# Reordering the chunks around the y transform, and splitting the turn of two transform results between ScalarE and VectorE

## The chip, the cores and the metric

The kernel runs on one core of a Trainium2 chip. The time is device microseconds (us) from the first to the last instruction of one launch, and the time of a kernel is the median of several runs. The engines go by short names: PE is TensorE (matrix products), ACT is ScalarE, DVE is VectorE, POOL is GpSimd, and SP is the engine whose queue issues most of the DMAs. SBUF is the on-chip working memory of 128 partitions; PSUM is the memory that PE writes its results into.

## The reference, cut to what matters

The program is a Fourier neural operator of four layers over 64 images of 256 x 256 points and 32 channels, and one transformer layer behind it. The change touches only the first three Fourier layers.

```python
v = x @ p_w + p_b                                  # 64 images, 32 channels, 256 x 256
for i in range(4):
    x_ft = rfft2(v)                                # only 24 x 12 modes are kept
    x1 = irfft2(x_ft[kept modes] mixed by W1, W2)
    x2 = einsum('bcxy,cd->bdxy', v, w_w[i]) + w_b[i]
    v = x1 + x2
    v = (v - mean(v)) * rsqrt(var(v) + eps) * bn_g[i] + bn_b[i]
    if i < 3: v = relu(v)
out = einsum('bcxy,cu->bxyu', v, q_w) + q_b        # then attention and a feed-forward layer
```

The kernel does the transforms as matrix products with tables of cosines and sines. The mean and variance of layer i+1 are worked out ahead of it: the variance needs the sum of squares of `v @ w_w[i+1]`, which is why each layer also computes that product and sums its squares.

## The kernel before, in words

`layer(i, ...)` is called for i = 0, 1, 2. It loops over the 64 images `b`, and for each over 8 chunks `t` of the image. Four kinds of work are in the loop:

- **A chunk**, `pre(b, t)`: 8 products (L624) expand the inverse x transform `y_[b]` along y into two PSUM tiles; for i > 0, 16 products of 32 x 32 (L635) add the previous layer's values, loaded as `vin`. ACT applies relu to the first tile (L642) and DVE to the second (L643), both into the SBUF tile `vo`. SP stores `vo` (L644). DVE turns `vo` in 32 x 32 blocks into half of a tile `t32` (L647).
- **A product**, `product(b, t)`: 16 products of 32 x 32 (L659) of `vo` with the next layer's weights into two PSUM tiles, whose squares ACT sums (L666).
- **The forward transform** of image b: `along_y(b)` reads all four `t32` tiles of the image in 128 products (L676) into two PSUM tiles, and DVE turns both into `zt` (L686). `along_x(b)` makes 12 products out of `zt` (L699), ACT copies the result (L706) and SP stores it.
- **The inverse x transform** of the next image: `scale_am(b + 1)` on POOL (L594) and `spread(b + 1)`: four products (L605) into two PSUM tiles, which DVE turns into `y_[b + 1]` (L609).

In the trace each product of the source shows as two matmuls, so a product over 16 tiles is 32 instructions, `along_y` 256, L624 of a chunk 16.

PE runs one stage behind: chunk t, then the product of chunk t - 1. `along_y(b - 1)` stands behind the product at t = 1 of image b, `along_x(b - 1)` behind the product at t = 3, `spread(b + 1)` behind that at t = 5.

**Buffers.** All PSUM tiles of the layer come from one pool of four tiles named `ring`[...]: a chunk takes two, a product two, `along_y` two, `along_x` one, `spread` two. `t32` tiles come from the pool `lt` of five; an image needs four of them. `vin` and `vo` have four buffers each, `zt` one:

```python
(n, k) for n, k in (("lo", 4), ("ly", 2), ("la", 2), ("lc", 1), ("lx", 2), ("lz", 1), ("lt", 5))
pp = pool("lp", 4, space=PSUM)
```

A tile whose buffers are all taken waits until the last reader of an earlier tile of the pool is done.

**Order.** The layer runs inside `with tc.manual_schedule():`, so each engine issues its instructions in the order in which the program emits them; only the waits set how the engines stand to one another. An instruction that waits on an engine holds back all that stand behind it there.

Of the kernel before, what the change touches and what calls it, by code (L numbers as in the profile page):

```python
# [9 lines left out]
F32 = mybir.dt.float32  # L10
# [7 lines left out]
C = 32  # L18
# [117 lines left out]
def tile_fno_fusion_transformer(ctx: ExitStack, tc: tile.TileContext, a, cst_d, grid_d, out):  # L136
    nc = tc.nc
# [370 lines left out]
    def layer(i, st, src, dst, acc):  # L508
# [7 lines left out]
        with ExitStack() as cx:  # L516
# [69 lines left out]
            def load_v(b, t):  # L586
                vin[b, t] = ip.tile([128, 8, S], F32, name="vin")
                nc.sync.dma_start(vin[b, t], src[b][:, t])
# [8 lines left out]

            def spread(b):

                y_[b] = yp.tile([128, 2, 32, C], F32, name="y_")  # L600
                for h in range(2):
                    ps = pp.tile([128, 2, 512], F32, name="ring")
                    for n in range(2):
                        hv = slice(64 * n, 64 * n + rows_)
                        nc.tensor.matmul(  # L605
                            ps[:, n, :], lhsT=EX[hv, 128 * h:128 * h + 128], rhs=ams[b % 2][hv],
                            start=True, stop=True, skip_group_check=True,
                        )
                    nc.vector.transpose(  # L609
                        y_[b][:, h].rearrange("p q c -> p c q"),  # L610
                        ps.rearrange("p n (c k) -> p (n c) k", k=32),
                    )

            def four():

                t2 = [pp.tile([128, 2, 512], F32, name="ring") for _ in range(2)]
                return t2, [t2[n // 2][:, n % 2] for n in range(4)]

            def pre(b, t):
                t2, ps = four()  # L620
                for r in range(2):
                    for n in range(4):
                        q = 8 * (t % 4) + 4 * r
                        nc.tensor.matmul(  # L624
                            ps[n][:, 256 * r:256 * r + 256],
                            lhsT=y_[b][32 * n:32 * n + K, t // 4, q:q + 4, :].rearrange("p q c -> p (q c)"),
                            rhs=mv[b % 2][32 * n:32 * n + K, 2 * t + r, :] if i == 0 else T4[32 * n:32 * n + K, :],
                            start=r == 0, stop=i == 0, skip_group_check=True,
                        )
                if i:  # L630
                    v = vin.pop((b, t))
                    for k in range(4):
                        for n in range(4):
                            j = (n + k) % 4
                            nc.tensor.matmul(  # L635
                                ps[n][32 * j:32 * j + 32], lhsT=ws[32 * n:32 * n + 32],
                                rhs=v[32 * n:32 * n + 32, 2 * j:2 * j + 2, :], start=False, stop=True,
                                skip_group_check=True, tile_position=(32 * n, 32 * j),
                            )
                o = vo[b, t] = op.tile([128, 8, S], F32, name="vo")  # L640
                of = o.rearrange("p (n r) y -> p n (r y)", r=2)
                nc.scalar.activation(of[:, 0:2], t2[0], AF.Relu)  # L642
                nc.vector.tensor_scalar(of[:, 2:4], t2[1], 0.0, None, ALU.max)  # L643
                nc.sync.dma_start(dst[b][:, t], o)  # L644
                if t % 2 == 0:
                    t32[b, t // 2] = tp.tile([128, 8, 16, C], F32, name="t32")
                nc.vector.transpose(  # L647
                    t32[b, t // 2][:, :, 8 * (t % 2):8 * (t % 2) + 8, :].rearrange("p y s c -> p s y c"),
                    o.rearrange("p s (y l) -> p s y l", l=32),
                )  # L650

            def product(b, t):

                o = vo.pop((b, t))
                t2, ps = four()
                for k in range(4):
                    for n in range(4):
                        j = (n + k) % 4
                        nc.tensor.matmul(  # L659
                            ps[n][32 * j:32 * j + 32], lhsT=w4[i + 1][32 * n:32 * n + 32],  # L660
                            rhs=o[32 * n:32 * n + 32, 2 * j:2 * j + 2, :], start=True, stop=True,
                            skip_group_check=True, tile_position=(32 * n, 32 * j),
                        )
                for n in range(2):
                    at = 2 * (8 * b + t) + n
                    nc.scalar.activation(t2[n], t2[n], AF.Square, accum_out=acc[:, at:at + 1])  # L666
# [3 lines left out]
            def along_y(b):  # L670
                t2, ps = four()
                for k in range(8):
                    for m in range(4):
                        for n in range(4):
                            j = (n + m) % 4
                            nc.tensor.matmul(  # L676
                                ps[n][32 * j:32 * j + 32], lhsT=FYT[32 * n:32 * n + 32, k, :],
                                rhs=t32[b, j][32 * n:32 * n + 32, k].rearrange("p s c -> p (s c)"),
                                start=k == 0, stop=k == 7, skip_group_check=True,
                                tile_position=(32 * n, 32 * j),  # L680
                            )
                for j in range(4):
                    t32.pop((b, j))
                zt = zts[b] = zp.tile([128, 2, 32, C], F32, name="zt")
                for h in range(2):
                    nc.vector.transpose(  # L686
                        zt[:, h].rearrange("p k c -> p c k"),
                        t2[h].rearrange("p n (s c) -> p c (n s)", c=C),
                    )

            def along_x(b):
# [21 lines left out]
                for t in range(4):  # L713
                    load_v(0, t)
            scale_am(0)
            spread(0)
            for b in range(B + 1):
                for t in range(8):
                    if b < B:
                        pre(b, t)  # L720
                        nb, nt = (b, t + 4) if t < 4 else (b + 1, t - 4)
                        if i and nb < B:
                            load_v(nb, nt)
                    pb, pt = (b, t - 1) if t else (b - 1, 7)
                    if pb >= 0 and (b < B or t == 0):
                        product(pb, pt)
                    if b and t == 1:
                        along_y(b - 1)
                    if b and t == 3:
                        along_x(b - 1)  # L730
                    if b + 1 < B:
                        if t == 0:
                            load_am(b + 1)
                            if i == 0:
                                load_x(b + 1)
                        if t == 2:
                            scale_am(b + 1)
                        if t == 5:
                            spread(b + 1)

    st = None
    acc = None
# [405 lines left out]
```

## Time and profile before

| what | value |
| --- | --- |
| median of 3 runs | 12365.77 us (12355.73 to 12369.66) |
| the profiled execution | 12360.58 us, its span 12358.8 us |
| PE busy | 11164.5 us, 90% of the span |
| DVE busy | 8774.8 us, 71% |
| ACT busy | 6094.5 us, 49% |
| PE, layer 0 (200 to 3062 us) | busy 2599.55 of 2862.00 us |
| PE, layer 1 (3205 to 6326 us) | busy 2875.70 of 3121.00 us |
| PE, layer 2 (6470 to 9600 us) | busy 2883.83 of 3130.00 us |
| DMA share in those layers | 0.54, 0.90, 0.90 |

A line of a timeline gives start, duration, engine, source line, operation, output<-inputs, shapes and count, and in brackets the idle time of the engine before it and what ended it. `PEld` is PE's weight load. A line of the groups gives the total busy time and the mean duration of one instruction in ns behind the bar, and then the idle time before the group. A matmul's end is modelled in the profile, and consecutive matmuls overlap, so that the distance from one start to the next says more than the duration of one.

### The profile page before, as it was taken

To read this page: it belongs to the slowest core of one execution; us is meant where nothing else is said; L and a number is where in the kernel's file an instruction comes from. 1 tells how busy PE (TensorE), PEld (TensorE's weight loads), DVE (VectorE), ACT (ScalarE), POOL (GpSimd) and SP (SyncE) were. 2 spreads that over 40 slices of the span, in tenths; PEclk is the share of its full clock that TensorE was granted. 3 is DMA by queue.
4 is the path that set the end of the run, shared out by engine and by line. 5 is a ranking of instruction groups with operands and counts; after the bars stand their busy time and mean duration, and the time that the engine had idled before them with its cause. 6 is when DMAs were issued, how large, how long until landed. Compare 5 with 4: busy or idle time off the path is not lost. (4 is left out here: it accounts for less than half of the span.)

```text
span 12358.8 us, 405064 instructions
## 1 busy us (share of the span) xinstructions
PE 11164.5 (90%) x182038; PEld 5874.0 (48%) x182038; DVE 8774.8 (71%) x10667; ACT 6094.5 (49%) x10249; POOL 1412.7 (11%) x1987
## 2 busy tenths in 40 slices
PE   6999999998799999999979999999999699999999
PEld 3444444443444444444434444444444366666666
DVE  6777777777776777777766777767777566666665
ACT  5555555555555555555544555555555333333333
POOL 0000000000000000000010000000000133333333
PEclk8999999999899999999989999999999799999999
DMA  7555555555899999888889989889899755555554
GB/s 226 200 199 203 203 201 201 201 200 210 325 354 349 349 351 350 348 347 348 346 302 352 354 346 355 339 339 353 346 351 352 247 234 227 219 228 233 218 223 152
DMA packets 589283, 3485.06 MB, mean 282 GB/s; under 512 B 95000, under 2 KB 144536, under 8 KB 188568
## 3 DMA queue, kind: packets, MB, share of 16 engines
q1 hardware_dynamic: 539520, 3392.84, 71.2%
q0 software_dynamic: 40880, 62.59, 2.0%
q8 instruction: 1423, 23.31, 0.8%
q10 hardware_dynamic: 7144, 3.72, 0.1%
q14 instruction: 316, 2.59, 0.1%
HBM read 1761.87 MB, written 1696.92 MB: 280 GB/s over the span
## 5 line engine op out<-in xcount | busy, mean ns | idle before, releaser
L666 ACT ACTIVATE ring<-ring 128x1024 f32<-128x1024 f32 x3072 | 3108.8, 1012 | 1186.4 <-PE ring L659 1148.7
L647 DVE STREAM_TRANSPOSE t<-vo 128x2048 f32<-128x2048 f32 x1536 | 3550.0, 2311 | 175.1 <-ACT vo L642 14.5
L659 PE MATMUL ring<-vo,w 32*32 32x512 f32 x49152 | 2849.3, 622 | 392.2 <-DVE zt L686 138.7
L642 ACT ACTIVATE vo<-ring 128x1024 f32<-128x1024 f32 x1536 | 1568.2, 1021 | 2997.7 <-PE ring L635 2378.9
L643 DVE TENSOR_SCALAR vo<-ring 128x1024 f32<-128x1024 f32 x1536 | 1857.7, 1209 | 608.2 <-PE ring L635 420.4
L676 PE MATMUL ring<-t,cst 32*32 32x512 f32 x49152 | 1864.7, 601 | 303.7 <-issue 302.1
L686 DVE STREAM_TRANSPOSE zt<-ring 128x1024 f32<-128x1024 f32 x384 | 711.8, 1925 | 1658.6 <-PE ring L676 1658.6
L659 PEld LDWEIGHTS ring<-vo,w 32*32 32x32 f32 x49152 | 761.3, 105 | 1898.7 <-ACT ring L666 477.0
L676 PEld LDWEIGHTS ring<-t,cst 32*32 32x32 f32 x49152 | 975.9, 103 | 1157.0 <-issue 707.8
L594 POOL TENSOR_TENSOR ams<-am,sk 48x512 f32<-48x512 f32 x384 | 486.9, 1268 | 8642.4 <-DMA am<-mix 8039.9
L635 PE MATMUL ring<-vin,ws 32*32 32x512 f32 x32768 | 1238.0, 606 | 22.1 <-issue 19.8
L699 PEld LDWEIGHTS ring<-cst,zt 128*128 128x128 f32 x4608 | 536.4, 194 | 174.6 <-ACT vo L642 161.6
L666 ACT ACTIVATION_READ_ACCUMULATOR ring<-ring 128x1 f32 x3072 | 584.1, 190 | 0.0
L1097 POOL DMA_DIRECT2D out_dram<-o x1024 | 504.4, 501 | 659.8 <-DVE o L1092 628.2
L699 PE MATMUL ring<-cst,zt 128*128 128x96 f32 x4608 | 568.7, 281 | 8.1 <-DVE zt L686 8.1
L896 PE MATMUL hp<-ch,win 128*32 128x512 f32 x4096 | 472.0, 601 | 8.3 <-DMA ch<-v 8.1
L635 PEld LDWEIGHTS ring<-vin,ws 32*32 32x32 f32 x32768 | 253.5, 103 | 407.9 <-issue 377.8
L605 PE MATMUL ring<-ams,cst 49*128 49x512 f32 (+1 forms) x1536 | 391.5, 621 | 37.6 <-POOL ams L594 27.2
L901 ACT ACTIVATE h<-hp,hbias 128x512 f32<-128x512 f32 x64 | 44.0, 687 | 595.5 <-PE hp L896 595.5
L419 PE MATMUL mps<-wm,xh 32*64 32x128 f32 (+1 forms) x4608 | 121.3, 374 | 203.4 <-ACT e L431 74.1
L1059 PE MATMUL pp<-zs,w 128*128 128x165 f32 x2048 | 302.1, 305 | 0.0
L1070 PE MATMUL pp<-g,w 128*128 128x165 f32 x2048 | 298.6, 303 | 0.0
(936 smaller groups left out, 11812.8 us busy)
## 6 DMA issues: line engine op xcount, KB each, us to landing
v<-vo SPq DMA_DIRECT2D x1536, 1024.0 KB
vin<-v SPq DMA_DIRECT2D x1024, 1024.0 KB
ch<-v SPq DMA_DIRECT2D x512, 1024.0 KB
mix<-ob SPq DMA_DIRECT2D x96, 512.0 KB
am<-mix SPq DMA_DIRECT2D x384, 96.0 KB
xin<-in_x_dram SPq DMA_DIRECT2D x16, 1024.0 KB
mv<-in_x_dram SPq DMA_DIRECT2D x256, 64.0 KB
out_dram<-o POOLq DMA_DIRECT2D x1024, 16.0 KB, 3.0
```

The lines of the kernel that those rows point to most:

```text
L594: nc.gpsimd.tensor_tensor(ams[b % 2][hv], a_[hv], sk[hv].rearrange("p c k -> p (c k)"), ALU.mult)
L635: nc.tensor.matmul(ps[n][32 * j:32 * j + 32], lhsT=ws[32 * n:32 * n + 32], rhs=v[32 * n:32 * n + 32, 2 * j:2 * j + 2, :], start=False, sto ...
L642: nc.scalar.activation(of[:, 0:2], t2[0], AF.Relu)
L643: nc.vector.tensor_scalar(of[:, 2:4], t2[1], 0.0, None, ALU.max)
L647: nc.vector.transpose(t32[b, t // 2][:, :, 8 * (t % 2):8 * (t % 2) + 8, :].rearrange("p y s c -> p s y c"), o.rearrange("p s (y l) -> p s ...
L659: nc.tensor.matmul(ps[n][32 * j:32 * j + 32], lhsT=w4[i + 1][32 * n:32 * n + 32], rhs=o[32 * n:32 * n + 32, 2 * j:2 * j + 2, :], start=Tru ...
L666: nc.scalar.activation(t2[n], t2[n], AF.Square, accum_out=acc[:, at:at + 1])
L676: nc.tensor.matmul(ps[n][32 * j:32 * j + 32], lhsT=FYT[32 * n:32 * n + 32, k, :], rhs=t32[b, j][32 * n:32 * n + 32, k].rearrange("p s c -> ...
L686: nc.vector.transpose(zt[:, h].rearrange("p k c -> p c k"), t2[h].rearrange("p n (s c) -> p c (n s)", c=C),)
L699: nc.tensor.matmul(ps[:, 0, 96 * g:96 * g + 96], lhsT=zt[:, h, k0:k0 + 4, :].rearrange("p k c -> p (k c)"), rhs=FX[:, h, 48 * r:48 * r + 9 ...
L896: nc.tensor.matmul(hp[32 * g:32 * g + 32], lhsT=win[:, 7 - t:39 - t], rhs=ch[:, g], start=False, stop=t == 7, skip_group_check=True,)
L1097: nc.gpsimd.dma_start(out[b, 64 * n + 16 * g:64 * n + 16 * g + 16].rearrange("(p t) d -> p t d", t=2), o[32 * g + 8 * n:32 * g + 8 * n + 8 ...
```

## The change

In `layer`, for every image but the first, the chunk at t = 2 moves ahead of `along_y(b - 1)`, and the products of chunks 0 and 1 move behind it. PE's order around the transform was chunk 1, product 0, `along_y`, chunk 2, product 1, chunk 3; it becomes chunk 1, chunk 2, `along_y`, product 0, product 1, chunk 3.

In `along_y` and in `spread` the second of the two PSUM tiles is now copied by ACT into an SBUF tile `half` (one new tile of 128 x 1024 in the pool `lz`), and DVE turns it from there. In `along_y` the turn stands where it stood. In `spread` it is handed on as a function, `late`, and emitted inside the next chunk, between that chunk's relu on DVE (L643) and the turn of its `vo` (L647). The pools are otherwise as before, `lt` with its five buffers among them. The end of the loop is written out after it instead of running an extra turn of the loop.

```diff
             def spread(b):
...
-                    nc.vector.transpose(
-                        y_[b][:, h].rearrange("p q c -> p c q"),
-                        ps.rearrange("p n (c k) -> p (n c) k", k=32),
-                    )
+                    if h == 0:
+                        nc.vector.transpose(
+                            y_[b][:, 0].rearrange("p q c -> p c q"),
+                            ps.rearrange("p n (c k) -> p (n c) k", k=32),
+                        )
+                half = zp.tile([128, 2, 512], F32, name="half")
+                nc.scalar.copy(half, ps)
+                return lambda: nc.vector.transpose(
+                    y_[b][:, 1].rearrange("p q c -> p c q"),
+                    half.rearrange("p n (c k) -> p (n c) k", k=32),
+                )
...
-            def pre(b, t):
+            def pre(b, t, between=None):
...
                 nc.sync.dma_start(dst[b][:, t], o)
+                if between is not None:
+                    between()
                 if t % 2 == 0:
                     t32[b, t // 2] = tp.tile([128, 8, 16, C], F32, name="t32")
                 nc.vector.transpose(
...
                 zt = zts[b] = zp.tile([128, 2, 32, C], F32, name="zt")
-                for h in range(2):
+                half = zp.tile([128, 2, 512], F32, name="half")
+                nc.scalar.copy(half, t2[1])
+                for h, s2 in enumerate((t2[0], half)):
                     nc.vector.transpose(
                         zt[:, h].rearrange("p k c -> p c k"),
-                        t2[h].rearrange("p n (s c) -> p c (n s)", c=C),
+                        s2.rearrange("p n (s c) -> p c (n s)", c=C),
                     )
...
-            spread(0)
-            for b in range(B + 1):
+            spread(0)()
+            def chunk(b, t, between=None):
+                pre(b, t, between)
+                nb, nt = (b, t + 4) if t < 4 else (b + 1, t - 4)
+                if i and nb < B:
+                    load_v(nb, nt)
+
+            for b in range(B):
+                late = None
                 for t in range(8):
-                    if b < B:
-                        pre(b, t)
...
-                    pb, pt = (b, t - 1) if t else (b - 1, 7)
-                    if pb >= 0 and (b < B or t == 0):
-                        product(pb, pt)
-                    if b and t == 1:
+                    chunk(b, t, late)
+                    late = None
+                    if b == 0 or t not in (1, 2):
+                        if b or t:
+                            product(*((b, t - 1) if t else (b - 1, 7)))
+                    elif t == 2:
                         along_y(b - 1)
+                        product(b, 0)
+                        product(b, 1)
...
                         if t == 5:
-                            spread(b + 1)
+                            late = spread(b + 1)
+            product(B - 1, 7)
+            along_y(B - 1)
+            along_x(B - 1)
```

## The prediction, made before the result was known

> **What bounds the kernel now.** I read the table by slices, then the costliest groups, the waits, the windows by layer, and the timeline of one image in layer 1. The change lives in three layers of 64 images, some 9100 of 12358.8 us. The groups give the prices:
>
> ```profile
> L666 ACT ACTIVATE ring<-ring 128x1024 f32<-128x1024 f32 x3072 | 3108.8, 1012 | 1186.4 <-PE ring L659 1148.7
> L647 DVE STREAM_TRANSPOSE t<-vo 128x2048 f32<-128x2048 f32 x1536 | 3550.0, 2311 | 175.1 <-ACT vo L642 14.5
> L643 DVE TENSOR_SCALAR vo<-ring 128x1024 f32<-128x1024 f32 x1536 | 1857.7, 1209 | 608.2 <-PE ring L635 420.4
> L686 DVE STREAM_TRANSPOSE zt<-ring 128x1024 f32<-128x1024 f32 x384 | 711.8, 1925 | 1658.6 <-PE ring L676 1658.6
> ```
>
> Per chunk DVE needs 1.21 + 2.31 us and some 0.16 us between instructions, 3.69 us; PE needs about 3.45 us and ACT 3.4 us (relu 1.02, two squares of 1.01 + 0.19). So in a run of chunks DVE is the bound, if narrowly. PE alone works in the y transform (L676), while DVE waits for it: 1658.6 us before L686. Whole layers, with columns us, then busy PE, PEld, DVE, ACT, POOL, clock, DMA share, GB/s:
>
> ```profile
> 200.00:3062.00 2862.00, 2599.55 (x42950) 1206.89 (x42944) 2213.13 (x1277) 1601.13 (x2622) 165.93 (x137) 0.95 0.54 203
> 3205.00:6326.00 3121.00, 2875.70 (x58906) 1361.66 (x58904) 2233.65 (x1266) 1619.56 (x2597) 162.24 (x135) 0.99 0.90 349
> ```
>
> Now the timeline of one image, first around the inverse transform's turns (L609), then around `along_y`:
>
> ```profile
> 5018.97 3.67 DVE L609 STREAM_TRANSPOSE y__53729<-ring 128x1024 f32<-128x1024 f32 x2
> 5022.52 1.18 DVE L643 TENSOR_SCALAR vo<-ring 128x1024 f32<-128x1024 f32 x1
> 5022.70 1.14 PE L659 MATMUL ring<-vo,w 32*32 32x512 f32 x28 [0.69 <-DVE y__53729 L609]
> ...
> 5026.20 1.22 DVE L643 TENSOR_SCALAR vo<-ring 128x1024 f32<-128x1024 f32 x1
> ...
> 5034.61 4.71 PE L676 MATMUL ring<-t,cst 32*32 32x512 f32 x130
> 5034.93 2.31 DVE L647 STREAM_TRANSPOSE t<-vo 128x2048 f32<-128x2048 f32 x1
> 5039.86 4.44 PE L676 MATMUL ring<-t,cst 32*32 32x512 f32 x126 [0.53 <-issue]
> 5044.23 0.69 PE L624 MATMUL ring<-cst,y__53729 24*128 24x256 f32 x2
> 5044.30 3.69 DVE L686 STREAM_TRANSPOSE zt<-ring 128x1024 f32<-128x1024 f32 x2 [7.07 <-PE ring L676]
> 5048.30 1.49 PE L659 MATMUL ring<-vo,w 32*32 32x512 f32 x32
> 5048.77 1.23 DVE L643 TENSOR_SCALAR vo<-ring 128x1024 f32<-128x1024 f32 x1 [0.78 <-PE ring L635]
> 5049.79 1.40 PE L624 MATMUL ring<-cst,y__53729 24*128 24x256 f32 x16
> ```
>
> DVE has nothing to do for 7.07 us, then product 1 waits on PE for both turns of `zt`. From the first L609 to the start of the next image's `along_y`, DVE runs without a gap: there it, not PE, sets the pace. From there to `spread` PE does.
>
> Read over images 2 to 61 of each layer in the timeline: from the first L686 to chunk 3's first L624 is on average 4.95 us in layer 0, 5.07 and 5.10 in layers 1 and 2. An `along_y` takes 8.6 us in layer 0, 11.6 and 11.7 in the others, where PE stops inside it for nothing that the profile names:
>
> ```profile
> PEld ring L676 <- issue: 707.8, 1004, 5.3
> PEld ring L659 <- DVE zt L686: 360.2, 295, 1.6
> ```
>
> [...] The page's instruction queue q8 moved 1423 packets, which is 364,076 PE instructions by 256; the stops inside `along_y` stand in the layers with DMA at 0.90[...].
>
> **The change part by part.** Call E the end of `along_y`.
>
> *Chunk 2 ahead of it.* Removed: product 0 (1.49 us of PE in layers 1 and 2). Added: chunk 2, L624 1.07 and L635 0.88 from start to start, with a short wait for the squares of the previous image's product 7, about 2.1 us. E comes 0.6 us later. In layer 0 nothing: `along_y` there already waits for the relu on DVE of chunk 1 (it starts at 1045.03 us, L643 ends at 1044.92), and that covers the chunk. Chunk 2's relus and its DMAs move too: ACT and DVE are free during `along_y`, and SP issues the store and a load earlier with nothing late behind them.
>
> *What chunk 2 puts on DVE.* DVE's order becomes relu 2, turn of `vo` 2 (L647), then the two turns of `zt`. That L647 writes a new `t32`, the sixth: four belong to image b - 1 until `along_y(b - 1)` has read them, the fifth is b's first. The pool has five. So L647 has to wait for E, and both turns of `zt` are queued behind it on DVE. Before, the order was the turns and then this L647. No row shows this wait; bounds are nothing, if a buffer were free, and the whole 2.31 us. I take the whole: the count of buffers is in the code, and DVE issues in emission order.
>
> *Behind E.* DVE: L647 from E + 0.07 to 2.38, the first turn of `zt` 1.92, until E + 4.3. ACT copies the second tile by E + 1.1 (1.02 us; ACT is idle). PE: product 0 until E + 1.5, product 1 starts on the tile that ACT freed and waits for the other until 4.35; its remaining 28 matmuls take 1.07 to the next chunk (after the same wait now, 4954.26 to 4955.33). Chunk 3 starts at E + 5.4 instead of 5.07: +0.35. Bounds: +0.8 if product 1 takes the tiles in the other order, and 1.5 us less if it could have other tiles. In layer 0, 1.0 replaces 1.07: E + 5.3 against 4.95, but along_x waits there for the relu behind the squares, so +0.2. The second turn of `zt` ends by 6.3, before chunk 3 asks DVE at 7.6; its price is covered.
>
> *The inverse transform.* PE gains: product 5 waits for one turn and ACT's copy, not for two turns, 1.3 us sooner. But DVE sets the pace here. From the first L609 to the second L643 is now 5026.20 - 5018.97 = 7.23 us. It becomes turn 1.88, relu 1.22, late turn 1.9, L647 2.31 and gaps of 0.27: 7.58, so +0.3 (the two turns back to back had overlapped by a tenth). The turn from SBUF is not in the trace: 1.25 us, L647's rate, is the low end, 1.9 the high one. I take 1.9, since its output has the same stride. The low end gives -0.3. ACT's copy (1.02) lies after the squares and before chunk 6's relu, 1 us clear of it.
>
> *Ends.* Image 0 and the end of a layer are as before; the first `spread` costs half a us more, three times.
>
> **The sum.** 63 images in each layer. Layers 1 and 2: 0.6 + 0.35 + 0.3 = 1.25 us, times 126 = 158. Layer 0: 0.2 + 0.1, since chunks there lose time to PE and ACT as well: 0.3 x 63 = 19. Together +177 on the profiled execution's 12360.6: 12538. Its span is 2 us less, the median of the runs 5 us more, so 12540 for a median.
>
> **Rivals.**
> 1. *The sixth `t32` does not hold DVE* (against: the five buffers). Then L647 hides under `along_y`, the first turn of `zt` starts at E, product 1 ends near E + 3.3: in layers 1 and 2, 0.6 - 1.75 + 0.3 = -0.85, times 126 = -107; in layer 0 about -1.7, times 63 = -107. 12150, and some 75 lower with the fast turn. It decides from where the first turn of `zt` starts less than 1.1 us after E, instead of 2.4. This is the faster side.
> 2. *The turn from SBUF takes 1.25 us.* Layers 1 and 2: 0.95 - 0.3 = 0.65, 82 us; layer 0 nothing. 12445. [...] Against: the stride of the write stays.
> 3. *The longer wait behind `along_y` gives the instruction fetch time to catch up.* `along_y` loses 11.6 - 8.6 = 3.0 us an image to these stops. Were a third of it saved, 126 us would go: 12410, near no change. Against: the stops come inside `along_y`, ahead of the wait.
> 4. *Chunk 2's load and store, now in `along_y`, slow the fetch.* Another 0.7 us an image, 88 us: 12630.
>
> **How the numbers follow.** The forecast 0.50, rival 1 0.13, rival 2 0.18, rival 3 0.12, rival 4 0.07. No change means within 0.2%, 25 us, which is what a measurement of this kernel can tell. Rival 3 spreads on both sides of that bound: half of it and more is within, a little below. Faster 0.15, same 0.10, slower 0.75. The range reaches from rival 3's low part to rival 4: 12360 to 12630; outside are rival 1, the part of 3 below 12360, and half of rival 4, some 0.19.
>
> **What would show it.** The L647 of chunk 2 starts at the end of L676, its idle time ended by PE L676, and the first L686 some 2.4 us later. Product 1 shows four matmuls, a gap, then 28. L609 shows single turns near 1.9 us with L643 between them, and DVE still without gaps from there to `along_y`. Images in layers 1 and 2 take 1.2 us longer than the 49.2 and 49.3 us of before, in layer 0 about 0.3 longer than 44.8. I am wrong if L647 of chunk 2 runs inside `along_y`, or if L676 as a whole gets shorter.

## The result, and the profile after

The changed kernel takes 12519.18 us (median of 4 runs, 12506.86 to 12526.16), the kernel before 12363.51 us (4 runs on the same chip): a ratio of 1.0125, 95% interval 1.0108 to 1.0143. It is slower by 156 us; the forecast was 12540. The profiled execution's span is 12515.0 us against 12358.8.

The costliest groups of the kernel after, the rows that answer to those shown of before (L647 is now L657, L643 is L651, L686 is L698, with the copy L696 ahead of it):

```profile
L657 DVE STREAM_TRANSPOSE t<-vo 128x2048 f32<-128x2048 f32 x1536 | 3544.6, 2308 | 1573.6 <-PE ring L686 1425.2
L651 DVE TENSOR_SCALAR vo<-ring 128x1024 f32<-128x1024 f32 x1536 | 1858.9, 1210 | 986.4 <-PE ring L643 752.7
L696 ACT COPY half<-ring 128x1024 f32<-128x1024 f32 x192 | 194.3, 1012 | 1955.0 <-PE ring L686 1955.0
L698 DVE STREAM_TRANSPOSE zt<-half 128x1024 f32<-128x1024 f32 x192 | 390.6, 2034 | 0.0
L698 DVE STREAM_TRANSPOSE zt<-ring 128x1024 f32<-128x1024 f32 x192 | 356.5, 1857 | 39.5 <-PE ring L686 39.5
```

Before, DVE's 1658.6 us of waiting for the y transform stood ahead of the turns of `zt`. Now 1425.2 us of it stand ahead of L657, the turn of a chunk's `vo`, and only 39.5 ahead of L698. L657 reads a `vo` that was ready long before and writes `t32`. L686 only reads `t32`, so the one thing for which L657 can wait there is a `t32` buffer. The table of waits (the waiting engine, tile and line, what ended the wait, then us in total, times and the longest) gives how often: 189 times, which is 63 images in three layers.

```profile
DVE t L657 <- PE ring L686: 1425.2, 189, 11.3
PEld ring L686 <- issue: 712.0, 1247, 5.3
PEld ring L669 <- DVE zt L698: 484.1, 189, 2.9
```

The timeline of one image of layer 1 around the end of `along_y` (L686), in order of time:

```profile
5086.91 0.66 PE L686 MATMUL ring<-t,cst 32*32 32x512 f32 x7
...
5087.66 2.31 DVE L657 STREAM_TRANSPOSE t<-vo 128x2048 f32<-128x2048 f32 x1 [8.83 <-PE ring L686]
5087.70 1.01 ACT L696 COPY half<-ring 128x1024 f32<-128x1024 f32 x1 [10.49 <-PE ring L686]
...
5088.77 0.14 PEld L669 LDWEIGHTS ring<-vo,w 32*32 32x32 f32 x4 [0.95 <-ACT half L696]
...
5089.90 1.85 DVE L698 STREAM_TRANSPOSE zt<-ring 128x1024 f32<-128x1024 f32 x1
...
5091.61 2.04 DVE L698 STREAM_TRANSPOSE zt<-half 128x1024 f32<-128x1024 f32 x1
...
5091.80 1.14 PE L669 MATMUL ring<-vo,w 32*32 32x512 f32 x28 [1.98 <-DVE zt L698]
5092.87 0.74 PEld L632 LDWEIGHTS ring<-cst,y__54135 24*128 24x128 f32 x16 [0.84 <-issue]
```

Product 1 (L669) begins on the tile that ACT freed, stops after four matmuls, and waits 1.98 us for the turn of `zt`, which itself stood 2.24 us behind L657 (5089.90 - 5087.66). Chunk 3 starts at 5092.87, 5.2 us after the turn L657 was released.

**Where the time went.** An image is a loop of three stretches: from chunk 1's first product to E, the end of `along_y`; from E to chunk 4; from chunk 4 to the next image's chunk 1. I took each from the timeline as a mean over images 2 to 61 of a layer (us). E is the end of the last matmul. The prediction measured two things otherwise: its 8.6 and 11.6 us for `along_y` run to the start of the last matmul (to E they are 9.22 and 12.23), and its 5.07 us to chunk 3 runs from the first turn of `zt` (from E it is 4.90).

| kernel | layer 0: image | chunk 1 to E | E to chunk 4 | to next chunk 1 | layer 1: image | chunk 1 to E | E to chunk 4 | to next chunk 1 | layer 2: image |
| --- | --- | --- | --- | --- | --- | --- | --- | --- | --- |
| before | 44.80 | 12.58 | 11.29 | 20.92 | 49.23 | 16.16 | 11.32 | 21.74 | 49.33 |
| after | 44.48 | 13.91 | 12.04 | 18.54 | 50.75 | 16.24 | 12.60 | 21.92 | 50.55 |

63 images times (-0.32 + 1.52 + 1.22) give +152 us of the 156.2 us between the two spans. Nearly all of the loss in layers 1 and 2 stands in one stretch, from E to chunk 4. Layer 0 even gains a little.

### The profile page after: what moved, and what is told of

Same layout as the page of the kernel before. It is cut to its first block, busy times and chain, and to the rows that moved or that the text cites. A ratio compares the mean times of both kernels' runs of the same rounds, so it can differ in the third digit from the quotient of the medians.

```text
span 12515.0 us, 405634 instructions
## 1 busy us (share of the span) xinstructions
PE 11096.7 (89%) x182038; PEld 5931.9 (47%) x182038; DVE 8770.6 (70%) x10667; ACT 6462.6 (52%) x10633; POOL 1414.1 (11%) x1987
## 3 DMA queue, kind: packets, MB, share of 16 engines
q8 instruction: 1423, 23.31, 0.7%
## 5 line engine op out<-in xcount | busy, mean ns | idle before, releaser
L657 DVE STREAM_TRANSPOSE t<-vo 128x2048 f32<-128x2048 f32 x1536 | 3544.6, 2308 | 1573.6 <-PE ring L686 1425.2
L676 ACT ACTIVATE ring<-ring 128x1024 f32<-128x1024 f32 x3072 | 3109.1, 1012 | 873.6 <-PE ring L669 793.0
L669 PE MATMUL ring<-vo,w 32*32 32x512 f32 x49152 | 2660.9, 634 | 477.9 <-DVE zt L698 311.5
L651 DVE TENSOR_SCALAR vo<-ring 128x1024 f32<-128x1024 f32 x1536 | 1858.9, 1210 | 986.4 <-PE ring L643 752.7
L650 ACT ACTIVATE vo<-ring 128x1024 f32<-128x1024 f32 x1536 | 1565.6, 1023 | 1137.2 <-PE ring L643 1076.8
L686 PE MATMUL ring<-t,cst 32*32 32x512 f32 x49152 | 1907.6, 605 | 268.9 <-issue 248.6
L669 PEld LDWEIGHTS ring<-vo,w 32*32 32x32 f32 x49152 | 770.2, 105 | 1776.5 <-issue 522.0
L686 PEld LDWEIGHTS ring<-t,cst 32*32 32x32 f32 x49152 | 970.5, 103 | 1125.3 <-issue 712.0
L643 PE MATMUL ring<-vin,ws 32*32 32x512 f32 x32768 | 1230.2, 626 | 5.2 <-DMA vin<-v 4.9
L696 ACT COPY half<-ring 128x1024 f32<-128x1024 f32 x192 | 194.3, 1012 | 1955.0 <-PE ring L686 1955.0
L711 PEld LDWEIGHTS ring<-cst,zt 128*128 128x128 f32 x4608 | 536.8, 194 | 200.6 <-ACT vo L650 177.4
L676 ACT ACTIVATION_READ_ACCUMULATOR ring<-ring 128x1 f32 x3072 | 584.0, 190 | 0.0
L711 PE MATMUL ring<-cst,zt 128*128 128x96 f32 x4608 | 569.0, 281 | 8.5 <-DVE zt L698 8.4
L643 PEld LDWEIGHTS ring<-vin,ws 32*32 32x32 f32 x32768 | 246.4, 104 | 367.6 <-issue 340.8
L698 DVE STREAM_TRANSPOSE zt<-half 128x1024 f32<-128x1024 f32 x192 | 390.6, 2034 | 0.0
L698 DVE STREAM_TRANSPOSE zt<-ring 128x1024 f32<-128x1024 f32 x192 | 356.5, 1857 | 39.5 <-PE ring L686 39.5
```

The lines of the kernel that those rows point to most:

```text
L643: nc.tensor.matmul(ps[n][32 * j:32 * j + 32], lhsT=ws[32 * n:32 * n + 32], rhs=v[32 * n:32 * n + 32, 2 * j:2 * j + 2, :], start=False, sto ...
L657: nc.vector.transpose(t32[b, t // 2][:, :, 8 * (t % 2):8 * (t % 2) + 8, :].rearrange("p y s c -> p s y c"), o.rearrange("p s (y l) -> p s ...
L669: nc.tensor.matmul(ps[n][32 * j:32 * j + 32], lhsT=w4[i + 1][32 * n:32 * n + 32], rhs=o[32 * n:32 * n + 32, 2 * j:2 * j + 2, :], start=Tru ...
L686: nc.tensor.matmul(ps[n][32 * j:32 * j + 32], lhsT=FYT[32 * n:32 * n + 32, k, :], rhs=t32[b, j][32 * n:32 * n + 32, k].rearrange("p s c -> ...
L698: nc.vector.transpose(zt[:, h].rearrange("p k c -> p c k"), s2.rearrange("p n (s c) -> p c (n s)", c=C),)
L711: nc.tensor.matmul(ps[:, 0, 96 * g:96 * g + 96], lhsT=zt[:, h, k0:k0 + 4, :].rearrange("p k c -> p (k c)"), rhs=FX[:, h, 48 * r:48 * r + 9 ...
```

## The experiments

Nine kernels were run, each against the kernel before on the same chip. They are given by their labels; the times are medians, the intervals 95%.

| kernel | time | ratio to before | image in layer 0, 1, 2 | layer 1: chunk 1 to E | E to chunk 4 | to next chunk 1 |
| --- | --- | --- | --- | --- | --- | --- |
| turn_behind | 12074.49 | 0.9770 (0.9756 to 0.9785) | 41.99, 48.50, 48.36 | 16.27 | 10.28 | 21.95 |
| order_only | 13219.44 | 1.0696 (1.0680 to 1.0712) | 47.80, 54.62, 54.50 | 17.24 | 15.74 | 21.63 |
| copies_only | 12124.41 | 0.9813 (0.9799 to 0.9828) | 42.61, 48.58, 48.55 | 15.12 | 11.47 | 21.99 |
| zt_copy_only | 12325.94 | 0.9975 (0.9967 to 0.9983) | 43.84, 49.44, 49.37 | 16.26 | 11.44 | 21.73 |
| double_product | 12486.03 | 1.0103 (1.0088 to 1.0118) | 44.20, 50.45, 50.60 | 16.20 | 12.22 | 22.03 |
| turn_late | 12074.06 | 0.9771 (0.9755 to 0.9787) | 41.97, 48.34, 48.35 | 16.20 | 10.30 | 21.84 |
| store_quarter | 12137.87 | 0.9819 (0.9799 to 0.9839) | 44.78, 46.77, 48.23 | 13.96 | 11.13 | 21.67 |
| order_turn | 12478.78 | 1.0106 (1.0091 to 1.0121) | 44.54, 50.44, 50.25 | 17.19 | 11.62 | 21.63 |
| late_both | 11985.09 | 0.9702 (0.9686 to 0.9718) | 41.79, 47.85, 47.76 | 15.09 | 10.72 | 22.04 |

### Taking the wait for the sixth buffer out: turn_behind

The changed kernel, with one instruction moved: the turn of chunk 2 is emitted behind the two turns of `zt`. The wait for the buffer then falls together with DVE's wait for `along_y`, which it has anyway.

```diff
-                if t % 2 == 0:
-                    t32[b, t // 2] = tp.tile([128, 8, 16, C], F32, name="t32")
-                nc.vector.transpose(...)
+                def turn():
+                    if t % 2 == 0:
+                        t32[b, t // 2] = tp.tile([128, 8, 16, C], F32, name="t32")
+                    nc.vector.transpose(...)
+                if b and t == 2:
+                    return turn
+                turn()
...
                         along_y(b - 1)
                         product(b, 0)
                         product(b, 1)
+                        turn()
```

> The changed kernel with one thing moved: chunk 2's turn of its vo (L657) is emitted behind the two turns of zt instead of ahead of them. Same work, same buffers, same waits. Theory (the sixth t32 holds DVE until the end of along_y, and the turns of zt stand behind it): the first turn of zt starts at the end E of along_y instead of E + 2.1, chunk 3's first product near E + 3.4 instead of E + 5.4 in layers 1 and 2; about 1.7 us an image less there and 1.5 in layer 0, in all some 310 us: 12210. Rival A (the loss comes from ACT's copies and from turning out of SBUF): within 30 us of the changed kernel's 12519. Rival B (the delayed turn of vo only moves the wait to chunk 3's relu on DVE): 12400 to 12480.

It took 12074.49 us, 445 us less than the changed kernel, and beats the kernel before by 2.3%. From E to chunk 4 layers 1 and 2 lost 2.3 us (12.60 to 10.28 and 10.31) and layer 0 2.5 (12.04 to 9.51), L657's 2.31 us or a little more. That is 136 us more than was expected. Chunk 3 starts about where it should (3.50 us behind E, expected 3.4); the rest is 0.45 us less from chunk 3 to `along_x` in layers 1 and 2 (4.39 to 3.93), and a layer 0 that gained 2.5 us instead of 1.5. DVE in one image of layer 1:

```profile
5100.65 1.95 DVE L702 STREAM_TRANSPOSE zt<-ring 128x1024 f32<-128x1024 f32 x1 [8.72 <-PE ring L690]
5102.45 2.05 DVE L702 STREAM_TRANSPOSE zt<-half 128x1024 f32<-128x1024 f32 x1
5104.40 2.25 DVE L658 STREAM_TRANSPOSE t<-vo 128x2048 f32<-128x2048 f32 x1
5106.58 1.18 DVE L651 TENSOR_SCALAR vo<-ring 128x1024 f32<-128x1024 f32 x1
```

The turn of `zt` is now released by the end of `along_y`, and L658 follows without a wait. So the wait for the sixth `t32`, with the turns of `zt` queued behind it, is the cause of the slowdown: without it the same change is a gain. The direct cure, a sixth buffer, was not tried.

### The parts by themselves: copies_only, order_only, order_turn

copies_only keeps the kernel's old order and takes both ACT copies and the late turn. order_only takes the new order and leaves both copies out; order_turn is order_only with chunk 2's turn moved as in turn_behind. Against the changed kernel, copies_only is

```diff
-                    if b == 0 or t not in (1, 2):
-                        if b or t:
-                            product(*((b, t - 1) if t else (b - 1, 7)))
-                    elif t == 2:
+                    if b or t:
+                        product(*((b, t - 1) if t else (b - 1, 7)))
+                    if b and t == 1:
                         along_y(b - 1)
-                        product(b, 0)
-                        product(b, 1)
```

and order_only is

```diff
-                half = zp.tile([128, 2, 512], F32, name="half")
-                nc.scalar.copy(half, t2[1])
-                for h, s2 in enumerate((t2[0], half)):
+                for h, s2 in enumerate(t2):
...
-                            late = spread(b + 1)
+                            spread(b + 1)
```

> The kernel before with the copies alone, the late turn of the inverse transform among them; the order of chunks and products is as before. Theory: the copies free the second tile 1.1 us after E and the first turn the other at E + 1.9, so product 1 has no wait for the second turn; chunk 3 starts at E + 3.5 instead of 4.9 in layers 1 and 2, less 0.25 for the late turn; layer 0 gains about 1 us: together some 200 to 260 us less than before, 12105 to 12165. Rival A (the copies are what costs): 12400 or more.

> The new order of chunks and products, without the copies: both transforms' results are turned out of PSUM as before. Theory: behind E, DVE does chunk 2's turn of vo (2.3 us) and two turns of zt, and product 1 needs both tiles, so chunk 3 starts near E + 7.2 instead of 5.4; 1.8 us an image more than the changed kernel, times 189 is 340, and layer 0 loses what it gained at the inverse transform, 55 us: 12880. Rival A (the copies are what costs): 12360 or less.

> The new order of the chunks with chunk 2's turn moved behind the turns of zt, as in turn_behind, but without ACT's copies: both second halves are turned by DVE from PSUM at once, as in the kernel before. Theory (the order is worth nothing by itself; what it brings comes from the copies, which free a PSUM tile early): product 1 waits for the two turns of zt until 3.7 us behind the end of along_y, chunk 3 starts 4.8 to 5.0 us behind it as in the kernel before (4.9), along_y ends 0.5 us later in layers 1 and 2, and the clock halves now and then after the wait of some 2 us: 12400 to 12560, taken 12480. Rival (the order hides work of its own, product 0 beside the turns): 12300 or less.

| | without copies | with copies |
| --- | --- | --- |
| old order | 12360 | 12124 (copies_only) |
| new order, turn of chunk 2 held by its buffer | 13219 (order_only) | 12519 (the changed kernel) |
| new order, turn of chunk 2 moved | 12479 (order_turn) | 12074 (turn_behind) |

copies_only came out at the expected number, the copies alone are worth 236 us, but not in the expected places, so the hit is in part luck. In layer 0, where about 1 us was expected, an image gains 2.19 us: the copies bring the next chunk 1 nearer (18.53 us from chunk 4, before 20.92), since product 5 no longer waits for two turns. In layers 1 and 2 the gain was to come behind E, and there is none: chunk 3 starts 0.8 and 0.95 us sooner, but from chunk 3 to `along_x` takes 4.52 and 4.54 us instead of 3.57, and chunk 4 starts 11.47 and 11.37 us behind E, before 11.32 and 11.33. Their 0.65 and 0.79 us an image come from ahead of E instead (16.16 to 15.12 and 16.26 to 15.04).

The order alone costs 859 us, 339 more than the expectation's 520, and the table says what of it is the buffer: 741 us without the copies (13219 - 12479), 445 with them. The order freed of the wait is worth little either way: 119 us slower without the copies, 50 faster with them. (order_turn ran on a chip where the kernel before took 12346 us; by the ratio the 119 are 131 us, and the 741 some 12 less.) order_turn hit its number, and its theory (the copies bring the gain) holds for the time. Chunk 3 starts where it was expected, 4.8 us behind E. But from chunk 1 to E layers 1 and 2 lost 1.0 us, twice the 0.5 that I had put there, and layer 0 gained 0.26.

order_only's waits show why it is so dear. Product 1 now stands behind L650 (the turn of `vo` in this kernel) and both turns of `zt` (L689):

```profile
DVE t L650 <- PE ring L679: 1513.7, 189, 12.3
DVE vo L644 <- PE ring L636: 1174.0, 302, 6.2
PEld ring L662 <- DVE zt L689: 947.5, 378, 4.0
```

PE's weight loads waited 947.5 us for the turns of `zt`, against 360.2 before and 484.1 after. By stretches (63 images times the differences in the three layers), 517 of the 859 us stand between E and chunk 3, which starts 7.55 to 7.77 us behind E; 125 stand ahead of E; and 239 between chunk 3 and `along_x`, where the work is the same (5.31 and 5.23 us in layers 1 and 2, before 3.57). The last part came to light in the clock.

### The clock after the wait: double_product

The same work on PE takes longer in some images of the changed kernel than in others. Of one image of layer 1, PE's timeline, and windows around it (us, busy PE, PEld, DVE, ACT, POOL, then the granted clock, DMA share and GB/s):

```profile
5192.58 1.29 PE L669 MATMUL ring<-vo,w 32*32 32x512 f32 x28 [1.99 <-DVE zt L698]
5193.80 2.09 PE L632 MATMUL ring<-cst,y__55325 24*128 24x256 f32 x16
5195.82 2.02 PE L643 MATMUL ring<-vin,ws 32*32 32x512 f32 x32
5197.53 2.40 PE L669 MATMUL ring<-vo,w 32*32 32x512 f32 x32
5199.87 3.10 PE L711 MATMUL ring<-cst,zt 128*128 128x96 f32 x24
```

```profile
5190.10:5193.50 3.40, 1.42 (x32) 0.23 (x28) 3.40 (x3) 1.59 (x4) 0.00 (x0) 0.99 0.81 342
5193.50:5200.30 6.80, 6.80 (x96) 2.73 (x83) 3.08 (x3) 3.49 (x6) 0.00 (x0) 0.50 0.08 33
5200.30:5203.70 3.40, 3.40 (x40) 3.22 (x39) 1.39 (x1) 2.10 (x5) 0.00 (x0) 1.00 0.99 304
```

After the wait of 1.99 us the clock is 0.50 for 6.80 us, then 1.00. Chunk 3 to `along_x` (L711) takes 6.07 us here (5193.80 to 5199.87), and 3.5 us in the image shown first, where the clock stayed at 1.00. Over images 2 to 61 of layers 1 and 2 of the changed kernel that stretch takes 5.04 us in the 65 images in which more than 0.3 us of it lie in low clock, and 3.60 and 3.56 us in the others; before, 3.57. So this split accounts for the mean rise of 0.8 us there (8.47 - 4.90 = 3.57 before, 9.73 - 5.35 = 4.38 after).

The wait ahead of a low stretch need not be long: before half of the changed kernel's low stretches PE had idled less than 1.92 us of the 3.41 us ahead of them, and in its three layers, of 167 waits of PE of 1.75 to 2.0 us 61% were followed by one within 7 us, of 173 waits of 0.25 to 0.5 us 3%.

The length of a wait alone doesn't decide, though: of the waits of 1.75 to 2.0 us inside `along_y`, 6 of 41 were followed by one in the kernel before, and none of 34 in turn_behind. The clock records show what goes with it. In each of the eleven traces the low stretches begin on one fixed grid of 3.413 us, to within 0.02 us over the whole run. Take PE's idle time (by the profile's modelled ends) in each interval of the grid at full clock, in the three layers. Of the changed kernel's intervals with less than 0.9 us idle, 1 of 1994 was followed by a low one, of those with 1.9 us or more 76 of 77; over all eleven traces it is 7 of 23426 and 457 of 479. In between it was 66 of 390 in the changed kernel, and what decides there is open. So it matters where a wait falls: of the changed kernel's waits of 1.75 to 2.0 us for the turn of `zt`, 43 of the 44 that lie inside one interval were followed by low clock, and 34 of the 72 that fall across two.

All low stretches together are 1145 us of the changed kernel's profile, 916 before, 2147 of order_only's, 694 of turn_behind's.

To try whether the clock follows the wait, double_product does product 0 twice behind `along_y`, which fills 1.1 us of PE's wait with work and leaves the rest as it was.

```diff
-            def product(b, t):
+            def product(b, t, times=1):
...
-                for k in range(4):
+                for k in list(range(4)) * times:
...
-                        product(b, 0)
+                        product(b, 0, 2)
```

> The changed kernel, with the 16 products of chunk 0 behind along_y done twice over into the same tiles with the same result: 32 more matmuls on PE per image, about 1.1 us, placed just ahead of the wait of product 1 for DVE. Theory (PE's waits of about 2 us behind along_y cost more than their length, since the granted clock halves after them): the wait of product 1 shrinks by the added work, so the start of chunk 3 stays where it was (5.35 to 5.45 us behind the end of along_y), chunk 3 to the start of along_x takes 9.0 to 9.3 us in layers 1 and 2 instead of 9.73 minus 5.35 = 4.4 us, that is 3.6 to 3.9 us, and the stretches of low clock fall well below the 143 of the changed kernel; 12519 - 126 x 0.6 = 12440, at most 12519, though PE does more. Rival (the clock has no part in it, chunk 3 is slow for its own waits): chunk 3 to along_x stays at 4.4 us, and the time stays at 12519 or rises by up to 126 x 0.3 = 40.

Low clock fell from 468 to 291 us in images 2 to 61 of layers 1 and 2, and the images there that lose time to it between chunk 3 and `along_x` went from 65 to 24 of 120. But neither the expected time nor the expected stretch came: 12486.03 us has an interval that overlaps the changed kernel's, and the stretch became 4.21 and 4.29 us, not 3.6 to 3.9. Its images without low clock now take 4.05 us where they took 3.6, since the matmuls of chunk 3 take 1.34 us from first to last against 0.85. The trace shows why: chunk 3 gets product 0's two tiles, and the second is free only when ACT has squared it, which comes later when product 0 is done twice. In 53 of those 96 images chunk 3 pauses behind its fourth matmul and goes on 0.1 to 0.2 us after one of these squares (L676) ends. The edit thus added a wait of its own. Still, PE can do 1.1 us more work per image at no cost in time, which says that the wait, not PE's work, sets the time here; that the low clock costs 0.8 us an image rests on the split of the images above.

### One copy alone: zt_copy_only

The kernel before, with ACT's copy and the turn from SBUF in `along_y` only.

```diff
-                for h in range(2):
+                half = zp.tile([128, 2, 512], F32, name="half")
+                nc.scalar.copy(half, t2[1])
+                for h, s2 in enumerate((t2[0], half)):
                     nc.vector.transpose(
                         zt[:, h].rearrange("p k c -> p c k"),
-                        t2[h].rearrange("p n (s c) -> p c (n s)", c=C),
+                        s2.rearrange("p n (s c) -> p c (n s)", c=C),
                     )
```

> The kernel before with only along_y's second tile copied by ACT and turned from SBUF; the inverse transform and the order as before. Theory: the gain behind along_y alone, 1.35 us an image in layers 1 and 2 (170 us), 0.4 in layer 0: 12170, so at most 65 us from copies_only. Rival A: 12364 or more. If layer 0's share of the copies lies at the inverse transform, layer 0 is 0.9 us an image slower here than in copies_only, and layers 1 and 2 are 0.25 faster.

A miss: 12325.94 us, 34 us less than before, not 190. Chunk 3 does start sooner, 4.26 us behind E in layer 1 instead of 4.90, but chunk 4 starts 11.44 us behind it, before 11.32. The timeline of one image, DVE and PE:

```profile
5098.40 2.01 DVE L691 STREAM_TRANSPOSE zt<-ring 128x1024 f32<-128x1024 f32 x1 [9.21 <-PE ring L679]
...
5100.26 2.04 DVE L691 STREAM_TRANSPOSE zt<-half 128x1024 f32<-128x1024 f32 x1
...
5102.11 1.27 DVE L644 TENSOR_SCALAR vo<-ring 128x1024 f32<-128x1024 f32 x1
5102.19 0.70 PE L625 MATMUL ring<-cst,y__55117 24*128 24x256 f32 x4
5103.43 1.13 PE L625 MATMUL ring<-cst,y__55117 24*128 24x256 f32 x12 [0.54 <-DVE vo L644]
```

PE no longer waits for the second turn of `zt`, but chunk 2's relu on DVE (L644 here) does: it runs at 5102.11, behind both turns, and chunk 3 waits for the tile that it frees. The copy has moved the wait by one step.

### Two ways to place DVE's work: turn_late and late_both

turn_late is turn_behind with chunk 2's turn emitted still later, in chunk 3 behind chunk 3's relu on DVE. late_both goes back to the old order and both copies (copies_only) and treats the second turn of `zt` as the change treats that of `y_`: it is emitted in chunk 2, between the relu and the turn of `vo`. Against copies_only it is

```diff
-                for h, s2 in enumerate((t2[0], half)):
+                def turn(h, s2):
                     nc.vector.transpose(
                         zt[:, h].rearrange("p k c -> p c k"),
                         s2.rearrange("p n (s c) -> p c (n s)", c=C),
                     )
+                turn(0, t2[0])
+                return lambda: turn(1, half)
...
-                        along_y(b - 1)
+                        late = along_y(b - 1)
```

> As turn_behind (12074), but the turn of chunk 2 is emitted in chunk 3, between chunk 3's relu on DVE and its own turn. Theory: in turn_behind the turn of chunk 2 still stands ahead of chunk 3's relu on DVE, which PE's next products wait for; moved behind that relu it delays nothing until the turns of chunk 3 and 4: 0.3 to 0.5 us an image in layers 1 and 2, little in layer 0: 12020 to 12050. Rival (DVE is the bound from there on and two turns in a row delay chunk 4's relu by the same 2.3 us): 12074, plus or minus 20.

> The order of the kernel before, with ACT's copies and the late turn of the inverse transform, as in copies_only (12124), and the second turn of zt late as well: it is emitted in chunk 2, between chunk 2's relu on DVE and its turn. Theory (in copies_only chunk 2's relu on DVE is queued behind two turns and holds the tile that chunk 3 needs): that relu ends 3.2 instead of 4.9 us behind the end of along_y, chunk 3 starts at 3.1 instead of 4.09 in layers 1 and 2, chunk 4 1.0 to 1.5 us sooner than 11.47, in layer 0 0.7 sooner than 10.26; with DVE the bound behind it 1.1 us an image in layers 1 and 2: 12124 - 126 x 1.1 - 63 x 0.7 = 11940. Rival (DVE's sum of work is the same, and what PE gains here it loses at the next relu): 12100 to 12124.

turn_late gave 12074.06 us, no change. That is the rival's number, but the traces don't show its reason. In layers 1 and 2 the turn was hardly in the way: chunk 3's relu on DVE starts 6.47 us behind E in turn_behind and 6.44 in turn_late (layer 1), both close behind the end of chunk 3's products on PE (6.21 and 6.24), and chunk 4's relu likewise follows PE (12.71 and 12.73, products 12.51 and 12.54), not the two turns. In layer 0 chunk 3's relu does start 1.26 us sooner, and chunk 4 starts no sooner for it (9.51 and 9.52).

late_both gave 11985.09 us, 3.0% below the kernel before, and is the fastest of all. The theory's direction holds, its size less: 139 us instead of 184. DVE in one image of layer 1:

```profile
5099.36 2.00 DVE L698 STREAM_TRANSPOSE zt<-ring 128x1024 f32<-128x1024 f32 x1 [8.79 <-PE ring L686]
5101.72 1.22 DVE L651 TENSOR_SCALAR vo<-ring 128x1024 f32<-128x1024 f32 x1 [0.35 <-PE ring L643]
5102.86 2.08 DVE L698 STREAM_TRANSPOSE zt<-half 128x1024 f32<-128x1024 f32 x1
5104.85 2.26 DVE L657 STREAM_TRANSPOSE t<-vo 128x2048 f32<-128x2048 f32 x1
```

The relu stands between the turns and starts 0.35 us after DVE came free. Layer 0 does what was expected (chunk 3 at 3.05 us behind E, chunk 4 0.86 sooner than in copies_only). In layers 1 and 2 chunk 3 starts 4.20 and 4.16 us behind E on average, hardly other than in copies_only, but chunk 4 0.75 and 0.70 sooner. The theory had the wrong tile of the two. Chunk 3's first matmuls go into the tile that chunk 2's relu on ACT frees: in 98 of 120 images they start within 0.15 us of that relu's end. The relu on DVE frees the second tile (in 100 of 120 images the fifth matmul starts within 0.15 us of its end), so the gain stands behind the start of chunk 3: from there to `along_x` takes 3.68 and 3.67 us, in copies_only 4.52 and 4.54.

### What stops PE inside `along_y`: store_quarter

In layers 1 and 2 PE stops inside `along_y` for nothing that the profile names. The prediction put this down to instructions that arrive late, and two of its rivals turned on it. store_quarter takes traffic away from layer 1.

```diff
-                nc.sync.dma_start(dst[b][:, t], o)
+                nc.sync.dma_start(dst[b][:, t, 0:2] if i == 1 else dst[b][:, t], o[:, 0:2] if i == 1 else o)
...
-                    nc.sync.dma_start(vin[b, t], src[b][:, t])
+                    if i == 2:
+                        for n in range(4):
+                            nc.sync.dma_start(vin[b, t][:, 2 * n:2 * n + 2], src[b][:, t, 0:2])
+                    else:
+                        nc.sync.dma_start(vin[b, t], src[b][:, t])
```

> The kernel before, with layer 1 storing only a quarter of each chunk of its result and layer 2 loading that quarter four times; it leaves out three quarters of layer 1's stores, so what follows layer 1 is not the reference's. DMA traffic in layer 1 falls from a share of 0.90 to about 0.6; in layer 2 it stays. Theory (the stops of PE inside along_y, which the profile puts down to nothing but issue, come from instructions that are fetched late because the DMA engines are busy): along_y in layer 1 falls from 12.2 us toward 9.2 to 10.5, its PE idle time put down to issue from 141 us to under 50, and an image of layer 1 from 49.2 to about 47 us; layer 2 stays at 49.3 and 12.3. Together about -140 us: 12220. Rival (PE outruns its own instruction supply in layers 1 and 2, whatever the DMA does): layer 1 stays at 12.2 and 49.2 us, and the time at 12360.

PE's stops inside `along_y` between 3300 and 6100 us, in layer 1, first before and then in store_quarter (L680 is `along_y` there):

```profile
PE ring L676 <- issue: 132.6, 92, 2.6
```

```profile
PE ring L680 <- issue: 44.9, 48, 2.3
```

The same stretch in store_quarter has a DMA share of 0.67 and 233 GB/s, before 0.90 and 348. An image of layer 1 falls from 49.23 to 46.77 us, 2.20 of the 2.46 us ahead of E (16.16 to 13.96), and `along_y` from 12.23 to 10.27 us. So in layer 1 most of these stops go away with the DMA traffic of the stores. That it is the fetch of instructions which the traffic delays was the author's guess: the page of the kernel before has a DMA queue of the kind "instruction" (q8: 1423 packets, 23.31 MB, 0.8% of the 16 DMA engines' span), but no run shows a fetch that came late. The expectation missed on layer 2, and so on the time, 12137.87 for 12220: layer 2 was to stay as it was, and it fell too, from 49.33 to 48.23 us, with its share at 0.94 and 357 GB/s. There the loads read one quarter four times. So the share alone doesn't decide; what else does is open.

## Why the prediction was right

**The wait.** Right, and shown in both traces in which the new order has the turn of chunk 2 in its place, the changed kernel's and order_only's. L657 waits for `along_y` in 189 images of 189; the turn of `zt` starts 2.21, 2.04 and 2.10 us behind E by layer (2.4 forecast), and in 180 of the 189 product 1 shows four matmuls, its longest gap, then 28. In 33 of the 189 L657 starts over 0.3 us ahead of E, so its buffer was free before the last matmul. Rival 1, that the sixth `t32` doesn't hold DVE, is what turn_behind makes true by other means. The rival had -0.85 us an image in layers 1 and 2 and -1.7 in layer 0; turn_behind has -0.73, -0.97 and -2.81.

**E to chunk 4 in layers 1 and 2.** The prediction had +0.35 us, for chunk 3. Chunk 3 came +0.45 and +0.49. Then chunk 3 to `along_x` lost another 0.81 and 0.78, which no step had. This is the term that was mis-sized, +1.28 for +0.35: after product 1's wait the clock is halved in about half of the images. The working took PE's rates from rows of before, where that stretch was almost free of low clock (4 images of 120).

**Chunk 1 to E.** +0.6 forecast, +0.08 and -0.17 measured. Two terms were off and cancel. The order costs 1.0 us, not 0.6 (order_turn, 17.19 against 16.16): 0.72 ahead of `along_y`, and 0.29 in it (12.23 to 12.52 us). The second part is what rival 4 said, at less than half its 0.7 us; that chunk 2's load and store cause it is not shown. The copies give 1.0 back (copies_only, 15.12): with PE ahead of DVE after `spread`, its wait moves from chunk 7 (chunk 6 to 7 takes 3.70 us, before 5.30) to chunk 1 (chunk 0 to 1 takes 5.27, before 3.64), just ahead of `along_y`, whose stops shrink. This is what rival 3 said of a longer wait, at another place than rival 3 had it: not behind `along_y`, but ahead of it. That instruction fetch catches up in this wait is argued, not shown. With it came one of the two signs that the prediction had named for being wrong: `along_y` as a whole got shorter in layers 1 and 2 (12.23 to 11.87 and 12.31 to 11.71 us), while in layer 0 it got longer (9.22 to 10.36).

**The inverse transform.** +0.3 forecast for DVE's chain, +0.09 measured (7.23 to 7.32 us from the first turn to the second relu). The timeline of one image:

```profile
5059.46 1.95 DVE L611 STREAM_TRANSPOSE y__54135<-ring 128x1024 f32<-128x1024 f32 x1
5061.56 1.22 DVE L651 TENSOR_SCALAR vo<-ring 128x1024 f32<-128x1024 f32 x1 [0.15 <-PE ring L643]
5062.70 1.97 DVE L617 STREAM_TRANSPOSE y__54135<-half 128x1024 f32<-128x1024 f32 x1
5064.52 2.29 DVE L657 STREAM_TRANSPOSE t<-vo 128x2048 f32<-128x2048 f32 x1
```

The late turn takes 1.97 us, so the choice of 1.9 against L647's rate was right, and rival 2 is out; `zt<-half` at 2034 ns, dearer than `zt<-ring` at 1857, says the same. The choice went by the stride of the write, 128 bytes in the code of L609 and L686, which took 3.67 us for two and 1925 ns for one of 128 x 1024 elements in the kernel before; L647, which writes runs of 32 elements, took 2311 ns there for 128 x 2048. That the stride is the reason was the author's estimate; no run varies it. The 0.27 us of gaps in the sum were wrong: consecutive DVE instructions start up to 0.15 us before the one ahead ends (L657 1.82 us after L617).

**Layer 0.** +0.3 forecast, -0.32 measured. The step said that chunks there "lose time to PE and ACT as well" and gave the inverse transform +0.1. It brought -2.38 us from chunk 4 to the next chunk 1: in layer 0 the wait of product 5 for two turns was on the path before, and ACT's copy removes it, as copies_only shows by itself (-2.39). Of this the y transform takes 2.08 back: 1.33 ahead of E, where PE, now early, waits for the relu on DVE, and 0.75 behind it. The first of the two is in the waits of the kernel after between 300 and 3000 us; before, the same wait was for ACT's relu and took 40.9 us:

```profile
PEld ring L686 <- DVE vo L651: 74.6, 61, 1.2
```

**The sum.** The mechanism that makes the change a loss was forecast; that the sum came so near is luck. For layers 1 and 2 together the forecast was 2.5 us an image and 2.74 came: 1.85 too little from E to chunk 4, 1.29 too much ahead of E and 0.30 too much for the inverse transform cancel. Layer 0 was 0.6 us off, which is 39 us the other way. By the median it is 156 us against 177.

## What to carry to other kernels

Before moving a producer ahead of the consumer of an earlier round, count the buffers of every pool that it writes: one that is short holds its engine in order, with everything behind it, and here that turned a gain of 2.3% into a loss of 1.25%. A turn or copy that nobody needs soon belongs behind the relu that frees a PSUM tile, where that relu would have to wait for it: in late_both this gave 139 us, in turn_late, where the relu waited for PE, nothing. The gain of a copy off the bound must be followed to the next instruction queued behind it. Where PE is to wait, count what the clock loses afterwards too; here one wait of 2 us could cost a further 1.5 (5.04 against 3.6 us for chunk 3 to `along_x`).

## What the runs showed of the hardware that was not expected

- The granted clock of PE went to 0.50 in stretches of 3.4 us or a multiple, on a fixed grid of 3.413 us. PE's idle time within one interval of the grid goes with it: 76 of 77 intervals with 1.9 us or more were followed by a low one in the changed kernel, 1 of 1994 with less than 0.9. In order_only all 97 waits of 3 to 5 us in images 2 to 61 were, and 2147 of its 13218.8 us are low.
- The turn of `zt` took longer from SBUF than from PSUM: 2034 against 1857 ns for the same 128 x 1024 elements, in copies_only 2035 against 1969.
- With a longer PE wait ahead of the y transform came a shorter transform in layers 1 and 2 (12.23 to 11.46 us in copies_only), and taking away three quarters of layer 1's stores took 1.96 us from it. What stops PE inside it is not shown.
